# Seven-product expert steps: the third product is added on the sixth, the seventh and fourth go into the next step

## The chip, the cores and the metric

The kernel runs on one core of a Trainium2 chip. The metric is the time of one execution on the device in microseconds. The kernel before was run three times: 957.39, 956.89 and 956.15 us, median 956.89.

A core has several engines, each with its own in-order stream of instructions: TensorE (PE in the profile, its weight loads PEld), VectorE (DVE), ScalarE (ACT), GpSimd (POOL) and SyncE (SP, which issues DMAs). They meet at semaphores. TensorE writes its results to PSUM, which has eight banks; here they are called A, B, C, E and D0 to D3.

## The reference

One layer: cross-attention, then a feed-forward block with eight experts, each behind a layer norm and a residual.

```python
x = x + attention(layernorm(x), ctx)          # x: 16 x 112 x 256, ctx: 16 x 375 x 256
n = layernorm(x)                              # 1792 tokens of 256
g = einsum('bsh,ehf->ebsf', n, w_gate)        # 8 experts, 256 -> 1024
u = einsum('bsh,ehf->ebsf', n, w_up)
h = silu(g) * u
expert_out = einsum('ebsf,efh->ebsh', h, w_down)   # 1024 -> 256
cw = softmax(n @ w_router) * softmax((n @ w_gating) / 0.1)
cw = cw / (sum(cw) + 1e-9)
x = x + einsum('ebsh,bse->bsh', expert_out, cw)
```

All experts are computed for all tokens, in float32.

## The kernel before

The attention takes the first 110 us or so; a list scheduler written into the kernel (class `Line`) orders it, together with the very first expert step. Everything after that is emitted in the order of the code below, engine by engine.

**Steps.** The expert stage is cut into 128 steps (L303): eight experts, two halves of the tokens (896 each), four slices of 256 hidden features, and for each a gate step (even n, `m == 0`) and an up step (odd n, `up`). A step multiplies a 256 x 256 block of weights with 256 x 896 activations. It does so with seven products of 128 x 128 by 128 x 448 in place of eight, from sums of blocks made earlier (Winograd's form). Every product (`prod`, L444) is three float32r matmuls, high part by high, low by high and high by low, so a step has 21 matmuls of 448 columns. With Pi for product i, the four result blocks (token half T, feature half F) are

- (0,0) = P1 + P2
- W = P1 + P6, and (0,1) = W + P5 + P3
- U = W + P7, and (1,1) = U + P5
- (1,0) = U + P4

**Where the sums are made.** Matmuls add up in PSUM, but W is wanted in two sums and P5 in two. P1 goes to bank A; ACT copies it to B (L646), where P6 is added, which makes W. ACT copies W on to bank E (L656), where P7 and then P4 are added. VectorE copies W to SBUF as `w16` (L658). P5 goes to C; ACT copies it to SBUF as `p5` (L652), and P3 is added in C. VectorE then makes `c12 = w16 + C` (L671) and `c22 = p5 + E` (L676). TensorE's order in a step is P1, P5, P4 of the step before, P6, P2, P3, P7.

**What follows a step's results.** A gate step's blocks go through SiLU on ACT (`silu`, L463). An up step's blocks are multiplied into those on VectorE (`hide`, L522), cast to a high part on ACT (`hhi`) and the rest is formed on VectorE as a low part (`hlo`); `keep_hidden` (L480) casts at once and leaves the low part for later, `leave` (L515) leaves both. `carry` holds what is left for later under a name, and `finish` (L470) emits it at a chosen place of a later step.

**Down matmuls.** An up step queues 14 groups of three matmuls of 256 columns for the down projection (`queue_downs`, L715), and the next up step emits them, 4, 4 and 6 at a time, after its own products (`fill`, L454). They add up in D0 to D3 over the four slices, and `gather` (L431) takes a finished bank to the output with the routing weight. Groups 1 to 6 of an up step read token blocks T = 0 alone; the seventh is the first to read T = 1.

**Weights.** `begin` (L498) and `due` (L402) issue the weight loads (SP) and make their sums and low parts (POOL) some steps ahead; `hi` casts high parts on ACT in up steps.

Step 0 is in the attention's schedule, steps 1 to 5 follow hand-written scripts (`early_step`, L527), and `step` (L639) emits steps 6 to 127. What step 5 leaves over is put into `carry` by `left_over` (L608).

Of the kernel before, what the change touches and what calls it, by code (L numbers as in the profile page):

```python
# [143 lines left out]
def kernel(  # L144
# [17 lines left out]
    nc = tc.nc  # L162
# [3 lines left out]
    E, _, FF = w_gate.shape  # L166
# [10 lines left out]
    N = HT // 2  # L177
# [15 lines left out]
    def f(t):  # L193
        return t.bitcast(F32)

    def psum(tag, name):
        return pspool.tile([P, 512], F32, tag=tag, name=name)
# [14 lines left out]
    def buf(tag, shape, name, dtype=F32):  # L212
        if tag in AHEAD:
            fpool.tile([P, AHEAD.pop(tag)], F32, tag=f"ahead_{tag}", name=f"ahead_{tag}", bufs=1)
        return fpool.tile(shape, dtype, tag=tag, name=name, bufs=BUFS[tag])
# [87 lines left out]
    steps = [(e, h, j, m) for e in range(E) for h in range(NH) for j in range(NJ) for m in range(2)]  # L303
    PER = 2 * NJ
# [38 lines left out]
    def load_hi(k, part, copy=nc.scalar.copy):  # L343

        if k not in wts:
            t = buf("w", [P, 2, 7, P], f"w{k}", FR)
            wts[k] = (t[:, 0], t[:, 1])
        d, w = wparts(k)[part]
        copy(wts[k][0][:, d], w)  # L349
# [27 lines left out]
    for k in range(NW):  # L377
        e, i = divmod(k, PER)
        if e == 0:
            if i < EARLY:  # L380
                continue
            n = i - 2
            if i > EARLY:
                plan(n - 2, "raw", k)
        else:
            n = 2 * PER * (e - 1) + PER + (1, 3, 5, 5, 7, 9, 11, 13)[i]
# [3 lines left out]
        if k == EARLY:  # L390
            n = 1
        plan(n, "hi" if k != EARLY else "ghi", k)
        plan(n + 1, "lo", k)
    for q in range(E * NJ):
# [3 lines left out]
        n = (4, 6, 8)[j - 1] if e == 0 else 2 * PER * (e - 1) + PER + 2 * j + 9  # L398
# [3 lines left out]
    def due(n, what, *more):  # L402
        for k in todo.pop((n, what), ()):
            {"raw": load_raw, "rawd": load_rawd, "t": load_t, "lo": load_lo, "d": load_d,
             "hi": load_hi, "ghi": load_hi_slow}[what](k, *more)
# [5 lines left out]
    def down_group():  # L411

        n, h, q, fi, t, hs, first, last = downs.pop(0)
        e = q // NJ
        if (h, e) not in banks:
            banks[(h, e)] = {}
        bk_ = banks[(h, e)]
        opening = t // 2 not in bk_
        if opening:
            gather(t // 2)  # L420
            bk_[t // 2] = psum(f"D{t // 2}", f"pd{h}_{e}_{t // 2}")
        pd = bk_[t // 2][:, (t % 2) * D : (t % 2 + 1) * D]
        for s, (a, w) in enumerate(PASSES):
            nc.tensor.matmul(  # L424
                pd, hs[a][:, t * P : (t + 1) * P], wds[q][w][:, fi, :],
                start=(opening and s == 0), stop=(last and s == 2), skip_group_check=True,
            )
        if last:
            done.setdefault(t // 2, []).append((h, e, t, pd))

    def gather(bank, some=False):  # L431

        size = min(2, NTT - 2 * bank)
        if len(done.get(bank, ())) < (1 if some else size):
            return
        for h, e, t, pd in done.pop(bank):
            tt = h * NTT + t
            nc.vector.scalar_tensor_tensor(
                acc[tt], pd, cw[:, tt, e : e + 1], acc[tt], op0=ALU.mult, op1=ALU.add
            )  # L440
            if e == E - 1:
                (nc.scalar if h == NH - 1 and t == NTT - 1 else nc.sync).dma_start(out_f[tt * P : (tt + 1) * P, :], acc[tt])

    def prod(n, ps, i, start, stop):  # L444
        e, h, j, m = steps[n]
        w_ = wts[e * PER + 2 * j + m]
        xi, wi = PROD[i]
        for s, (w, a) in enumerate(PASSES):
            nc.tensor.matmul(  # L449
                ps, w_[w][:, wi, :], (xs_hi, xs_lo)[a][h][xi],  # L450
                start=(start and s == 0), stop=(stop and s == 2), skip_group_check=True,
            )

    def fill(k):  # L454
        for _ in range(min(k, len(downs))):
            down_group()
# [3 lines left out]
    def tmp(tag, n):  # L460
        return buf(tag, [P, N], f"{tag}_{n}")

    def silu(n, blk, src, own=True):  # L463
        s = src if own else tmp("s", f"{n}s{blk[0]}")
        nc.scalar.activation(s, src, AF.Silu)
        sg[blk] = s

    carry = {}

    def finish(*names):  # L470

        for name in names:
            if name in carry:
                carry.pop(name)()

    def parts(hid, blk):
        T, F = blk
        return [t[:, T * N : (T + 1) * N] for t in hid[F]]

    def keep_hidden(hid, blk):  # L480

        hi, lo = parts(hid, blk)
        s = sg[blk]
        nc.scalar.copy(hi, s)
        carry["hlo%d%d" % blk] = lambda: nc.vector.tensor_sub(lo, s, f(hi))
# [3 lines left out]
    def offer(n=1):  # L489

        while n and waiting:
            try:
                next(waiting[0])
                n -= 1
            except StopIteration:
                waiting.pop(0)

    def begin(n):  # L498

        for what in ("lo", "raw", "rawd", "t", "ghi"):  # L500
            due(n, what)
        hi_now = todo.pop((n, "hi"), ())

        def hi(part):
            for k in hi_now:
                load_hi(k, part)

        hid = None
        if n % 2:
            hid = [  # L510
                (buf("hhi", [P, HT], f"hhi{n}_{F}", FR), buf("hlo", [P, HT], f"hlo{n}_{F}", FR)) for F in range(2)
            ]
        return hi, hid

    def leave(hid, blk):  # L515

        hi, lo = parts(hid, blk)
        s = sg[blk]
        carry["hhi%d%d" % blk] = lambda: nc.scalar.copy(hi, s)
        carry["hlo%d%d" % blk] = lambda: nc.vector.tensor_sub(lo, s, f(hi))  # L520

    def hide(blk, src):  # L522
        nc.vector.tensor_mul(sg[blk], sg[blk], src)
# [115 lines left out]
    def step(n):  # L639
        e, h, j, m = steps[n]  # L640
        up = m == 1
        hi, hid = begin(n)

        pa, pb, pc = (psum(t, f"p{t}{n}")[:, :N] for t in "ABC")
        prod(n, pa, 1, True, False)
        nc.scalar.copy(pb, pa)  # L646
        if up:
            gather(2)
            gather(3)
        prod(n, pc, 5, True, False)  # L650
        p5 = tmp("v1", f"{n}p5")
        nc.scalar.copy(p5, pc)  # L652
        finish("fourth")
        prod(n, pb, 6, False, True)
        pe = psum("E", f"pE{n}")[:, :N]
        nc.scalar.copy(pe, pb)  # L656
        w16 = tmp("v1", f"{n}w")
        nc.vector.tensor_copy(w16, pb)  # L658
        finish("silu11")
        if up:  # L660
            due(n, "d")
        prod(n, pa, 2, False, True)
        if up:
            hide((0, 0), pa)
        else:
            silu(n, (0, 0), pa, False)
            finish("hhi01", "hhi11", "hhi10")
            due(n, "d")
        prod(n, pc, 3, False, True)
        c12 = tmp("s", f"{n}c12")  # L670
        nc.vector.tensor_add(c12, w16, pc)  # L671
        if not up:
            silu(n, (0, 1), c12)
        prod(n, pe, 7, False, False)
        c22 = tmp("s", f"{n}c22")
        nc.vector.tensor_add(c22, p5, pe)  # L676

        def fourth():
            prod(n, pe, 4, False, True)
            if up:  # L680
                hide((1, 0), pe)
                leave(hid, (1, 0))
            else:
                silu(n, (1, 0), pe, False)

        carry["fourth"] = fourth
        if up:
            keep_hidden(hid, (0, 0))
            hide((0, 1), c12)
            hide((1, 1), c22)  # L690
            fill(4)
            keep_hidden(hid, (0, 1))
            gather(0)
            finish("hlo00")
            hi(0)
            fill(4)
            if n == len(steps) - 1:
                finish("fourth")
            keep_hidden(hid, (1, 1))
            hi(1)  # L700
            gather(1)

            if n % PER != 1:
                finish("hlo01")
            offer(6)
            fill(6)
            queue_downs(n, hid)
        else:
            carry["silu11"] = lambda: silu(n, (1, 1), c22)
            finish("hlo00", "hlo01", "hlo11", "hlo10")  # L710
            hi(0)
            hi(1)
            offer(6)
# [618 lines left out]
    w16 = add("w", "v1", "B", "v1", ("first", "B"), waits=tail_s)  # L1332
# [5 lines left out]
    c22 = add("c22", "u", "C", u3, ("first", "C"))  # L1338
# [3 lines left out]
    c12 = add("c12", "w", "C", u3, c21, ("first", "C"), c22)  # L1342
# [40 lines left out]
    for n in range(1, len(steps)):  # L1383
# [7 lines left out]
            left_over(n, LEFT)  # L1391
        offer()
        assert not waiting
    finish("hlo01", "hlo11", "hhi10", "hlo10")
    while downs:
        down_group()
        for bank_ in range(4):
# [38 lines left out]
```

## Time and profile before

| | before |
|---|---|
| median of three runs | 956.89 us |
| the profiled execution | 957.04 us, span 955.3 us |
| TensorE busy | 948.3 us, 99% |
| VectorE busy | 655.5 us, 69% |
| ScalarE busy | 608.3 us, 64% |
| GpSimd busy | 377.4 us, 40% |
| copy of W to SBUF (L658) | 122 of 128 x 448, about 0.62 us each |
| copy of A to B (L646) | 122, 522 ns each |
| copy of B to E (L656) | 122, 517 ns each |

The span is the time from the first to the last instruction of the profiled execution; 1.7 us lie around it. A matmul of the expert stage starts 0.20 us after the one before it (448 columns) or 0.11 us (256 columns), while its own row is longer, since matmuls overlap. The trace's granted clock for TensorE is 0.999 of full speed. A row of the timeline gives start, duration, engine, line, operation and tiles; a bracket at its end says how long the engine had been idle and what ended that.

### The profile page before, as it was taken

To read this page: it belongs to the slowest core of one execution; us is meant where nothing else is said; L and a number is where in the kernel's file an instruction comes from. 1 tells how busy PE (TensorE), PEld (TensorE's weight loads), DVE (VectorE), ACT (ScalarE), POOL (GpSimd) and SP (SyncE) were. 2 spreads that over 40 slices of the span, in tenths; PEclk is the share of its full clock that TensorE was granted. 3 is DMA by queue.
4 is the path that set the end of the run, shared out by engine and by line. 5 is a ranking of instruction groups with operands and counts; after the bars stand their busy time and mean duration, and the time that the engine had idled before them with its cause. 6 is when DMAs were issued, how large, how long until landed. Compare 5 with 4: busy or idle time off the path is not lost.

```text
span 955.3 us, 16149 instructions
## 1 busy us (share of the span) xinstructions
PE 948.3 (99%) x6076; PEld 893.4 (94%) x6076; DVE 655.5 (69%) x1303; ACT 608.3 (64%) x1236; POOL 377.4 (40%) x481
## 2 busy tenths in 40 slices
PE   8999999999999999999999999999999999999998
PEld 5888999999999999999999999999999999999998
DVE  5878687777576666666575757667666767566675
ACT  5767776666666665666656666666666666666553
POOL 3437973344324433444244332543244431544000
PEclk9999999999999999999999999999999999999999
DMA  8621101011101110011101110111001110100001
GB/s 232 184 70 43 60 23 34 23 34 45 34 12 34 34 45 23 22 35 35 34 23 34 34 34 23 34 34 34 23 23 34 45 34 12 34 23 12 23 17 39
DMA packets 36577, 38.78 MB, mean 41 GB/s; under 512 B 3650, under 2 KB 34500, under 8 KB 36500
## 3 DMA queue, kind: packets, MB, share of 16 engines
q1 hardware_dynamic: 35808, 37.37, 13.3%
q8 instruction: 47, 0.77, 0.3%
q10 hardware_dynamic: 692, 0.40, 0.1%
q14 instruction: 30, 0.25, 0.1%
HBM read 34.08 MB, written 1.84 MB: 38 GB/s over the span
## 4 chain that ended last, share of the span: by engine, by line
PE 96%; DMA 1%; DVE 1%; ACT 1%; issue 0%; SPq 0%; ACTq 0%; DVEq 0%
PE pd L424 32%; PE pE L449 16%; PE pC L449 16%; PE pA L449 15%; PE pB L449 8%; PE ps_aa L1101 2%; PE ps_sc L1067 2%; PE ps_po L1116 1%; PE ps_cT L1055 1%; DMA wv<-in_L_xattn_Wv_dram 1%; PE ps_qk L1009 1%; PE ps_lg L1196 1%; PE ps_pp L1088 1%; DMA wn<-in_L_xattn_Wq_dram 0%; PE ps_xx L1163 0%
## 5 line engine op out<-in xcount | busy, mean ns | idle before, releaser
L424 PE MATMUL pd<-wd,hhi 128*128 128x256 f32 x1792 | 309.9, 277 | 0.0
L424 PEld LDWEIGHTS pd<-wd,hhi 128*128 128x128 f32 x1792 | 275.3, 188 | 2.0
L424 PE MATMUL pd<-wd,hlo 128*128 128x256 f32 x896 | 248.2, 277 | 0.4 <-DVE hlo L592 0.3
L449 PE MATMUL pC<-xs_hi,w 128*128 128x448 f32 x508 | 184.5, 363 | 0.0
L449 PE MATMUL pE<-xs_hi,w 128*128 128x448 f32 x508 | 184.1, 362 | 0.0
L359 POOL TENSOR_TENSOR w<-raw,w 128x384 fp32r<-128x384 f32 x64 | 78.3, 1223 | 265.3 <-ACT w L349 265.3
L449 PE MATMUL pA<-xs_hi,w 128*128 128x448 f32 x504 | 183.0, 363 | 0.0
L424 PEld LDWEIGHTS pd<-wd,hlo 128*128 128x128 f32 x896 | 168.3, 188 | 0.8 <-DVE hlo L592 0.8
L646 ACT COPY pB<-pA 128x448 f32<-128x448 f32 x122 | 63.6, 522 | 102.7 <-PE pA L449 102.7
L368 POOL TENSOR_TENSOR wd<-rawd,wd 128x512 fp32r<-128x512 f32 x32 | 41.8, 1306 | 182.0 <-ACT wd L366 182.0
L449 PEld LDWEIGHTS pC<-xs_hi,w 128*128 128x128 f32 x508 | 95.3, 188 | 10.4 <-DVE s_90c L671 0.4
L449 PEld LDWEIGHTS pE<-xs_hi,w 128*128 128x128 f32 x508 | 95.3, 188 | 6.3
L449 PEld LDWEIGHTS pA<-xs_hi,w 128*128 128x128 f32 x504 | 94.6, 188 | 5.5
L656 ACT COPY pE<-pB 128x448 f32<-128x448 f32 x122 | 63.1, 517 | 54.1 <-DVE s_4s L622 0.8
L449 PE MATMUL pC<-xs_lo,w 128*128 128x448 f32 x254 | 92.0, 362 | 0.0
L449 PE MATMUL pE<-xs_lo,w 128*128 128x448 f32 x254 | 91.8, 361 | 0.0
L449 PE MATMUL pB<-xs_hi,w 128*128 128x448 f32 x252 | 91.3, 362 | 0.0
L449 PE MATMUL pA<-xs_lo,w 128*128 128x448 f32 x252 | 90.9, 361 | 0.0
L359 POOL TENSOR_TENSOR w<-tt,w 128x512 fp32r<-128x512 f32 x64 | 88.5, 1382 | 0.0
L449 PEld LDWEIGHTS pE<-xs_lo,w 128*128 128x128 f32 x254 | 47.6, 187 | 3.3
L449 PEld LDWEIGHTS pB<-xs_hi,w 128*128 128x128 f32 x252 | 47.3, 188 | 3.1
L449 PEld LDWEIGHTS pC<-xs_lo,w 128*128 128x128 f32 x254 | 47.6, 187 | 2.5
(1456 smaller groups left out, 1779.0 us busy)
## 6 DMA issues: line engine op xcount, KB each, us to landing
raw<-in_L_ffn_w_gate_dram SPq DMA_DIRECT2D x32, 256.0 KB, 2.7
raw<-in_L_ffn_w_up_dram SPq DMA_DIRECT2D x32, 256.0 KB, 2.7
rawd<-in_L_ffn_w_down_dram SPq DMA_DIRECT2D x32, 256.0 KB, 2.7
ctx<-in_ctx_dram SPq DMA_DIRECT2D x13, 336.0 KB
out_dram<-acc SPq DMA_DIRECT2D x13, 128.0 KB, 1.7
wide<-in_ctx_dram SPq DMA_DIRECT2D x3, 336.0 KB, 7.5
wide<-in_x_dram SPq DMA_DIRECT2D x2, 448.0 KB
ctx<-in_ctx_dram SPq DMA_DIRECT2D x13, 39.0 KB
```

The lines of the kernel that those rows point to most:

```text
L359: nc.gpsimd.tensor_sub(wts[k][1][:, d], w, f(wts[k][0][:, d]))
L368: nc.gpsimd.tensor_sub(wds[q][1], rawds[q], f(wds[q][0]))
L424: nc.tensor.matmul(pd, hs[a][:, t * P : (t + 1) * P], wds[q][w][:, fi, :], start=(opening and s == 0), stop=(last and s == 2), skip_group_ ...
L449: nc.tensor.matmul(ps, w_[w][:, wi, :], (xs_hi, xs_lo)[a][h][xi], start=(start and s == 0), stop=(stop and s == 2), skip_group_check=True,)
L646: nc.scalar.copy(pb, pa)
L656: nc.scalar.copy(pe, pb)
L1009: nc.tensor.matmul(bank(("qk", g, m, 0), [P, GT]), m_b[k][a][:, m * P : (m + 1) * P], xnT_b[k][w], start=(k == 0 and s == 0), stop=(k == K ...
L1055: nc.tensor.transpose(bank(("cT", b, k), [P, TK])[:, c * KT : (c + 1) * KT], ct()[:, c, k * P : (k + 1) * P], ident[:KT, :KT],)
L1067: nc.tensor.matmul(bank(("sc", b), [TQ, TK]), own(qk_b[k], ("qk", g, k))[:, i * TQ : (i + 1) * TQ], ctT(k), start=(k == 0), stop=(k == KC ...
L1088: nc.tensor.transpose(bank(("pp", b), [KT, NK, TQ])[:, c, :], p()[:, c * KT : (c + 1) * KT], ident[:TQ, :TQ])
L1101: nc.tensor.matmul(bank(("aa", b), [P, KC, TQ])[:, k, :], ct()[:, c, k * P : (k + 1) * P], pT()[:, c, :], start=(c == 0), stop=(c == NK - 1),)
L1116: nc.tensor.matmul(bank(("po", b), [TQ, D]), aT()[:, a, k, :], (wv_hi, wv_lo)[w][:, k, :], start=(k == 0 and s == 0), stop=(k == KC - 1 an ...
```

## The change

P3 is added in bank B, on P1 + P6, instead of in C on P5. So `c12` becomes `p5 + B`, and the copy `w16` is gone. The bank that held P5 is then free: the copy of W goes there, and P7 and P4 are added there. This one bank, Z, is C in even steps and E in odd ones, so that P7 and P4 of a step can wait until the next: P7 is now emitted after the next step's P1 (with `c22` and what follows it), P4 before the next step's P3. TensorE's order is P1, P7 of the step before, P5, P6, P2, P4 of the step before, P3.

With them move the instructions that depend on them: the SiLU of (0,1) goes from the end of the gate step into the up step; the multiply and cast of (1,1) go from the up step into the next gate step; the casts and low parts of (1,0) and (1,1) go to the gate step after, or into the up step after that; gathers of D2 and D3 go from after P1 to after P6. The low part of (0,1) is always made in its own step. In the last step P7, P4 and what depends on them are emitted between the down groups.

```diff
@@ -639,75 +639,83 @@
     def step(n):
         e, h, j, m = steps[n]
         up = m == 1
+        end = n == len(steps) - 1
         hi, hid = begin(n)
 
-        pa, pb, pc = (psum(t, f"p{t}{n}")[:, :N] for t in "ABC")
+        pa, pb = (psum(t, f"p{t}{n}")[:, :N] for t in "AB")
         prod(n, pa, 1, True, False)
         nc.scalar.copy(pb, pa)
+        finish("silu01")
+        if up:
+            finish("hlo11")
+        finish("seven")
+        pz = psum("CE"[n % 2], f"pZ{n}")[:, :N]
+        prod(n, pz, 5, True, False)
+        p5 = tmp("v1", f"{n}p5")
+        nc.scalar.copy(p5, pz)
+        prod(n, pb, 6, False, True)
+        nc.scalar.copy(pz, pb)
+        finish("silu11")
         if up:
             gather(2)
             gather(3)
-        prod(n, pc, 5, True, False)
-        p5 = tmp("v1", f"{n}p5")
-        nc.scalar.copy(p5, pc)
-        finish("fourth")
-        prod(n, pb, 6, False, True)
-        pe = psum("E", f"pE{n}")[:, :N]
-        nc.scalar.copy(pe, pb)
-        w16 = tmp("v1", f"{n}w")
-        nc.vector.tensor_copy(w16, pb)
-        finish("silu11")
-        if up:
+            finish("hhi10")
             due(n, "d")
         prod(n, pa, 2, False, True)
         if up:
             hide((0, 0), pa)
+            finish("hlo10")
         else:
             silu(n, (0, 0), pa, False)
-            finish("hhi01", "hhi11", "hhi10")
+            finish("hhi11", "hlo00", "hlo01")
             due(n, "d")
-        prod(n, pc, 3, False, True)
+        finish("fourth")
+        prod(n, pb, 3, False, True)
         c12 = tmp("s", f"{n}c12")
-        nc.vector.tensor_add(c12, w16, pc)
-        if not up:
-            silu(n, (0, 1), c12)
-        prod(n, pe, 7, False, False)
-        c22 = tmp("s", f"{n}c22")
-        nc.vector.tensor_add(c22, p5, pe)
+        nc.vector.tensor_add(c12, p5, pb)
+
+        def seventh():
+            prod(n, pz, 7, False, False)
+            c22 = tmp("s", f"{n}c22")
+            nc.vector.tensor_add(c22, p5, pz)
+            if up:
+                hide((1, 1), c22)
+                leave(hid, (1, 1))
+            else:
+                carry["silu11"] = lambda: silu(n, (1, 1), c22)
 
         def fourth():
-            prod(n, pe, 4, False, True)
+            prod(n, pz, 4, False, True)
             if up:
-                hide((1, 0), pe)
+                hide((1, 0), pz)
                 leave(hid, (1, 0))
             else:
-                silu(n, (1, 0), pe, False)
-
-        carry["fourth"] = fourth
+                silu(n, (1, 0), pz, False)
+
+        carry.update(seven=seventh, fourth=fourth)
         if up:
             keep_hidden(hid, (0, 0))
             hide((0, 1), c12)
-            hide((1, 1), c22)
+            if end:
+                finish("seven", "hlo00")
             fill(4)
             keep_hidden(hid, (0, 1))
             gather(0)
             finish("hlo00")
             hi(0)
+            if end:
+                finish("hhi11", "fourth", "hlo01")
             fill(4)
-            if n == len(steps) - 1:
-                finish("fourth")
-            keep_hidden(hid, (1, 1))
             hi(1)
             gather(1)
-
-            if n % PER != 1:
-                finish("hlo01")
+            finish("hlo01")
+            if end:
+                finish("hhi10", "hlo11", "hlo10")
             offer(6)
             fill(6)
             queue_downs(n, hid)
         else:
-            carry["silu11"] = lambda: silu(n, (1, 1), c22)
-            finish("hlo00", "hlo01", "hlo11", "hlo10")
+            carry["silu01"] = lambda: silu(n, (0, 1), c12)
             hi(0)
             hi(1)
             offer(6)
@@ -1391,7 +1399,6 @@
             left_over(n, LEFT)
         offer()
         assert not waiting
-    finish("hlo01", "hlo11", "hhi10", "hlo10")
     while downs:
         down_group()
         for bank_ in range(4):
```

## The prediction

> **What bounds the kernel now.** I read the page's busy shares and its chain of waits first, to learn which engine sets the end.
>
> ```profile
> PE 948.3 (99%) x6076; PEld 893.4 (94%) x6076; DVE 655.5 (69%) x1303; ACT 608.3 (64%) x1236; POOL 377.4 (40%) x481
> ...
> PE 96%; DMA 1%; DVE 1%; ACT 1%; issue 0%; SPq 0%; ACTq 0%; DVEq 0%
> ```
>
> TensorE is busy throughout, and the chain that ends last is TensorE's own. A busy TensorE can still hide small gaps, so next comes the chain in order of time, in the middle of the expert stage.
>
> ```profile
> 479.04 4.78 PE pd L424 x42
> 483.82 0.60 PE pA L449 x3
> 484.42 0.60 PE pC L449 x3
> ...
> 488.02 0.61 PE pA L449 x3
> 488.63 0.60 PE pC L449 x3
> ...
> 491.63 0.61 PE pE L449 x3
> 492.24 4.79 PE pd L424 x42
> ```
>
> One pair of steps (gate and up) is 14 products of three matmuls and 42 down matmuls: 13.20 us from 479.04 to 492.24. Fourteen products at 0.60 and 4.78 for the downs give 13.18. So a pair holds about 0.02 us that is not matmul cadence. Over the whole stage the down groups start at 135.80 and, 60 pairs later, at 928.21: 13.207 each, so 0.027 x 60 = 1.6 us is all that better waiting could give back there. The changed function emits steps 6 to 127, 61 pairs. TensorE's list of waits confirms it; nothing in it belongs to these steps:
>
> ```profile
> PE ps_idle L815 <- DVE nhalf L223: 1.2, 1, 1.2
> PE ps_vb L923 <- ACT wide L1019: 1.0, 1, 1.0
> ...
> PE pd L424 <- DVE hlo L592: 0.3, 1, 0.3
> ```
>
> Last, the timeline from gate step 60 into up step 61, to see how late a result may come without delaying TensorE:
>
> ```profile
> 500.85 0.62 DVE L671 TENSOR_TENSOR s_60c<-v_60w,pC 128x448 f32<-128x448 f32 x1
> 501.07 0.36 PE L449 MATMUL pA<-xs_hi,w 128*128 128x448 f32 x1
> ...
> 501.46 0.37 PE L449 MATMUL pA<-xs_hi,w 128*128 128x448 f32 x1
> 501.51 0.58 ACT L465 ACTIVATE s_60c<-s_60c 128x448 f32<-128x448 f32 x1 [0.44 <-DVE s_60c L671]
> 501.67 0.37 PE L449 MATMUL pC<-xs_hi,w 128*128 128x448 f32 x1
> ...
> 501.99 0.53 ACT L646 COPY pB<-pA 128x448 f32<-128x448 f32 x1
> ...
> 502.88 0.36 PE L449 MATMUL pB<-xs_hi,w 128*128 128x448 f32 x1
> ```
>
> VectorE's sum over bank C ends at 501.47; the product that overwrites C starts at 501.67, 0.21 after the one before instead of 0.20. So **a result that ends 0.20 us ahead of its matmul is just in time**; this is the tightest edge of the old order. The copy into B ends at 502.52, 0.36 ahead of product 6, and costs nothing.
>
> **The change part by part.**
>
> *Removed:* the copy of B to SBUF (L658), 122 x 0.62 = 76 us of VectorE. It lies beside matmuls: 0 on the path. VectorE's cover falls from 69% to about 61%, so nothing is late next there.
>
> *TensorE's work:* the same 21 matmuls a step and 42 downs a pair, with the same weights: 0.
>
> *The new order, up step.* I lay it out from rows of before: product 0.60; a reader starts 0.40 after the start of a product's last matmul (501.46 would give 501.86; the first copy of a pair, matmul at 510.46 and copy at 510.86, shows it undisturbed); ACT 0.53, VectorE 0.62 with the next start 0.53 later; VectorE to ACT 0.04 to 0.09 (501.47 to 501.51; 512.68 to 512.77). Zero is the start of product 1; the order is 1, 7 of the gate step, 5, 6, 2, 4 of the gate step, 3.
> - Product 6 at 1.80 needs the copy A to B, and this now waits for the gate step's sum over B (product 3 has moved into B). Product 4's multiply on VectorE starts at -0.40 and lets go at 0.13; the sum runs 0.20 to 0.82, the copy 0.91 to 1.44. That is 0.36 ahead, 0.16 to spare, as before. Queued behind the copy on ACT are a SiLU and the copy of product 5, wanted only at 2.0.
> - Product 3 at 3.60 overwrites B, so it needs the copy B to bank Z: 2.60 to 3.13, 0.47 ahead.
> - Product 4 at 3.00 needs the sum after product 7 read: VectorE has the low-part subtraction first (0.73 to 1.35), then 1.40 to 2.02: 0.98 ahead. Even if that subtraction takes the 1.35 us that it takes in a few steps (481.87), the sum ends at 2.7, still 0.3 ahead.
> - The seventh down group, at 4.20 + 6 x 0.34 = 6.25, is the first to read the previous pair's low part of block (1,0), moved into this step behind its cast (3.6 to 4.15 on ACT): 4.20 to 4.82, over 1.4 ahead. A weight cast that shares this place (0.61 on ACT) comes after it in the queue.
> - The next gate step starts 4.8 us of downs later, with everything done. In it the SiLU on A (3.2 to 3.75) precedes the up step's product 1 at 4.20: 0.45 ahead, as now.
>
> So no edge is tighter than 0.36, and the edge at 0.20 (sum over C, then product 5) is gone, since C and E alternate. It costs 0.01 in each of 61 up steps, 0.6 us, and once more: from 699.46 to 700.18 two matmul starts are 0.41 and 0.31 apart instead of 0.20, 0.3 us, behind a late sum of step 90. **Gain 0.9 us**, bounds 0 and 1.6.
>
> *Step 6* is the first new step; it has no product 7 to issue, and its product 4 has moved back. So product 6 comes at 1.20, but the copy A to B runs 0.80 to 1.33 and wants 0.20 more: **0.33 us lost, once**.
>
> *The last step.* Product 7 ends at 4.80, four down groups follow, and product 4, moved ahead of the next four, would start at 6.17. VectorE must first do the low part (to 4.82), the sum over B (4.73 to 5.35), a multiply (5.26 to 5.87) and only then read Z, 5.79 to 6.41; plus 0.20, product 4 starts at 6.61: **0.44 us lost, once** (bounds 0 and 1.0, a further VectorE row or none in the queue). Ten down groups (3.4 us) then cover its multiply, cast and subtraction; the tail after them is as before.
>
> *Moved gathers, multiplies, SiLUs and casts:* each keeps its engine and its row, 0 on the path. In the 4.2 us of products ACT then has 5 instructions in a gate step and 7 in an up step, about 2.5 and 3.4 us, and VectorE 4 to 6, 2.1 to 3.2 us; the rest of an up step's work lies in 4.8 us of downs. Behind the low part at 4.20 VectorE's sum over B waits until 4.73, and behind that a multiply and a cast for the next pair. No DMA issue moves, and the SP and POOL queues keep their order.
>
> *A wait-only instruction on TensorE.* In the built program product 6 of each gate step from 8 on, 60 in all, is preceded by one, as it waits for VectorE and ACT. The expert stage of before has none, but the attention stage does:
>
> ```profile
> L1101 PEldq EVENT_SEMAPHORE  x1: 51/51/51, 31.5 to 31.5; - x1
> ```
> ```profile
> 31.44 1.49 PE L1101 MATMUL ps_aa<-s,ctx 125*128 125x112 f32 x12
> ```
>
> Upper bound 60 x 0.051 = 3.1 us. But these 12 matmuls, with the wait among them, start every (1.49 - 0.275) / 11 = 0.110 us, as the 24 at 25.56 do (2.67 us in all, 0.104 to 0.111 each). I take 0, by this nearest row; a product's matmul, at 0.20, leaves more room than one at 0.11. What the instruction waits for, VectorE's sum of the step before, ended more than 3 us earlier.
>
> [...]
>
> **The sum:** -0.9 + 0.33 + 0.44 = -0.13. The profiled execution took 957.04 us (span 955.3), 0.15 over the median of the three runs; so 956.9 against its own time and 956.8 as a median.
>
> **The rivals.** 0.2% (1.9 us) is about what a measurement of this kernel can tell from no change: below 955.0 or above 958.8.
> - *Product 6 of the up step comes late* (slower). Place: sum over B, copy A to B, product 6. It has 0.16 us to spare and decides from there: 0.20 beyond just-in-time (a sum that starts 0.36 late) gives 61 x 0.20 = 12 us, 969; a little over 0.03 is enough for 1.9 us. For it: two engines now follow each other between product 3 and product 6. Against it: both rows are fixed in length, 0.62 and 0.53, and the old order had the same 0.36.
> - *The 60 wait-only instructions are paid* (slower): 3.1 us, 959.8; from 0.03 each it counts. Against it: the row above.
> - *More is given back* (faster): all 1.6 us of the pairs and neither loss gives 955.3, still inside 0.2%. Beyond it the matmul cadence itself (0.200 and 0.113) would have to shrink. For it: 76 us less VectorE reading of PSUM beside the matmuls. Against it: product 1 takes 0.60 both at 483.82, where VectorE has nothing of its step to do yet, and at 488.02, amid its sums.
> - *76 us come off*, or a part of them, if VectorE were the bound: excluded by TensorE's 99%.
>
> **How the numbers follow.** No measurable change 0.70; late product 6 0.12 and paid waits 0.08, so slower 0.20; faster 0.10. Range: down to 955.0 (the 1.6 us and the noise: the three runs lie within 1.2 us); up to 960.2, past the paid waits. Left out are the late product 6 and most of the faster case, 2 in 10. Without rivals of either sign the forecast alone is 955.3 to 958.2: the bounds 0 and 1.6 on the gain, 0 and 1.3 on the two losses.
>
> **What would show it.** Right: pairs of 13.18 to 13.20 us between down groups; no L658 row; an idle gap before product 6 in step 6 and before product 4 in the last step, some 0.3 to 0.45 each; VectorE near 580 us busy. Wrong: pairs of 13.23 or more, and a gap before pB in up steps (late copy) or in gate steps (paid waits). What would make it wrong is a VectorE or ACT instruction that lasts longer in its new place than in its old one, ahead of the copy into B.

## The result: 0.1 to 0.3% slower, not the same

In the first comparison the changed kernel took 959.5 us (median of 8 executions, 958.19 to 961.46), the kernel before 956.39 (8 executions, 955.75 to 957.39): ratio 1.0027, 95% interval 1.0018 to 1.0037. The prediction said 956.8, range 955.0 to 960.2: the time lies in the range, but the likeliest case was no measurable change, and this is slower. A second comparison (below) gave 1.0015, 1.0002 to 1.0027. One remark is needed to read these: in some executions of every kernel that was run more than once the granted clock has a mean of 0.998 or 0.996, not 1.0, and they are 1.5 to 3 us longer; a single execution of the kernel before, 1754.59 us at a mean of 0.79, is left out everywhere.

The profiled execution of the changed kernel took 959.34 us, span 957.6 (before: 957.04 and 955.3). The page's busy shares and the shares of its chain of waits:

```profile
PE 950.8 (99%) x6076; PEld 898.4 (94%) x6076; DVE 619.3 (65%) x1181; ACT 598.1 (62%) x1236; POOL 378.4 (40%) x481
...
PE 96%; DMA 1%; DVE 1%; ACT 1%; issue 0%; SPq 0%; ACTq 0%; DVEq 0%
```

TensorE is the bound as before. Its own busy time is 2.5 us longer with the same 6076 matmuls, which is already a hint that it is not only waits that came. The chain in order of time, one pair of the changed kernel (start, length, what):

```profile
480.23 4.81 PE pd L424 x42
485.04 0.60 PE pA L449 x3
485.64 1.20 PE pZ L449 x6
486.84 0.60 PE pB L449 x3
...
492.84 0.60 PE pB L449 x3
493.44 4.81 PE pd L424 x42
```

The order is the new one (A, then 7 of the step before and 5 into Z, then B), and no product is longer than 0.60. But the 42 downs take 4.81 us where the rows of before have 4.78 and 4.79. A pair is 13.21 us. TensorE's list of waits has one new row:

```profile
PE ps_idle L823 <- DVE nhalf L223: 1.2, 1, 1.2
...
PE pd L424 <- DVE hlo L592: 0.3, 1, 0.3
PE pZ L449 <- DVE s_127c L680: 0.2, 1, 0.2
```

That is product 4 of the last step, as predicted. The other predicted loss, in step 6, is in the timeline (the bracket gives the idle time ahead and what ended it):

```profile
142.24 0.52 ACT L647 COPY pB<-pA 128x448 f32<-128x448 f32 x1 [0.19 <-PE pA L449]
...
142.44 0.37 PE L449 MATMUL pZ<-xs_hi,w 128*128 128x448 f32 x1
142.81 0.19 PEld L449 LDWEIGHTS pB<-xs_hi,w 128*128 128x128 f32 x1 [0.37 <-ACT pB L647]
142.81 0.47 PE L449 MATMUL pB<-xs_hi,w 128*128 128x448 f32 x1
```

Product 6 starts 0.37 after the matmul ahead of it in place of 0.20, and the next start is 0.11 late as well (0.31 in place of 0.20): 0.28 us. That is 0.05 behind the end of the copy (142.76) for the first start and 0.36 for the second.

**Where the 2.2 us between the two spans lie.** From the starts of the matmuls in both traces: the first product of the expert stage starts at 104.18 us, not 103.18, so 1.0 comes in the attention stage, which the change doesn't touch. From step 6 to the last matmul it is 812.87 us, not 811.56, so 1.31 comes in the steps that it does touch. The steps between and what follows the last matmul differ by less than 0.1. The 1.31 in parts, each a sum of distances between neighbouring starts (a gap is the lateness of a start that is over 0.03 us late):

| step 6 to the last matmul | before | after | difference |
|---|---|---|---|
| 2562 product matmuls, without gaps | 513.20 | 512.57 | -0.62 |
| 2520 down matmuls of the steps | 287.27 | 288.57 | +1.30 |
| gaps in products (before: at 699; after: 0.28 in step 6, 0.06 at 161, 0.21 at 305) | 0.32 | 0.55 | +0.23 |
| end: gaps | 0.34 | 0.80 | +0.46 |
| end: 87 matmuls | 10.44 | 10.38 | -0.05 |

(The rounded parts add up to 1.32.)

So two questions stood: is the 1.0 us in the attention stage the change's doing, and why do the same downs take 1.3 us longer?

### The profile page after: what moved, and what is told of

Its sections match the earlier page's. It is cut to its first block, busy times and chain, and to the rows that moved or that the text cites. A ratio compares the mean times of both kernels' runs of the same rounds, so it can differ in the third digit from the quotient of the medians.

```text
span 957.6 us, 16027 instructions
## 1 busy us (share of the span) xinstructions
PE 950.8 (99%) x6076; PEld 898.4 (94%) x6076; DVE 619.3 (65%) x1181; ACT 598.1 (62%) x1236; POOL 378.4 (40%) x481
## 4 chain that ended last, share of the span: by engine, by line
PE 96%; DMA 1%; DVE 1%; ACT 1%; issue 0%; SPq 0%; ACTq 0%; DVEq 0%
PE pd L424 32%; PE pZ L449 23%; PE pA L449 15%; PE pB L449 15%; PE ps_aa L1109 2%; PE ps_sc L1075 2%; PE ps_po L1124 1%; PE ps_cT L1063 1%; DMA wv<-in_L_xattn_Wv_dram 1%; PE ps_qk L1017 1%; PE ps_lg L1204 1%; PE ps_pp L1096 1%; DMA wn<-in_L_xattn_Wq_dram 0%; PE ps_xx L1171 0%; PE pE L449 0%
## 5 line engine op out<-in xcount | busy, mean ns | idle before, releaser
L449 PE MATMUL pZ<-xs_hi,w 128*128 128x448 f32 x732 | 246.2, 363 | 0.2 <-DVE s_127c L680 0.2
L449 PE MATMUL pB<-xs_hi,w 128*128 128x448 f32 x496 | 180.3, 363 | 0.0
L449 PEld LDWEIGHTS pZ<-xs_hi,w 128*128 128x128 f32 x732 | 137.4, 188 | 9.5 <-DVE s_127c L680 0.4
L449 PE MATMUL pZ<-xs_lo,w 128*128 128x448 f32 x366 | 131.8, 360 | 0.0
L449 PE MATMUL pB<-xs_lo,w 128*128 128x448 f32 x248 | 89.3, 360 | 0.0
L449 PEld LDWEIGHTS pZ<-xs_lo,w 128*128 128x128 f32 x366 | 68.4, 187 | 4.8
L657 ACT COPY pZ<-pB 128x448 f32<-128x448 f32 x122 | 63.1, 517 | 15.1 <-PE pB L449 0.4
L438 DVE SCALAR_TENSOR_TENSOR acc<-pd,cw,acc 128x256 f32<-128x256 f32 x112 | 48.3, 475 | 3.3 <-PE pd L424 3.3
L449 PEld LDWEIGHTS pA<-xs_lo,w 128*128 128x128 f32 x252 | 47.1, 187 | 2.5
L449 PEld LDWEIGHTS pB<-xs_lo,w 128*128 128x128 f32 x248 | 46.4, 187 | 3.2
```

The costliest lines, as they stand in the source:

```text
L438: nc.vector.scalar_tensor_tensor(acc[tt], pd, cw[:, tt, e : e + 1], acc[tt], op0=ALU.mult, op1=ALU.add)
L449: nc.tensor.matmul(ps, w_[w][:, wi, :], (xs_hi, xs_lo)[a][h][xi], start=(start and s == 0), stop=(stop and s == 2), skip_group_check=True,)
L657: nc.scalar.copy(pz, pb)
```

## The experiments

There are ten runs beside the first comparison: both kernels once more and eight variants, in three sessions, each on its own chip with its own executions of the kernel before.

### The attention stage: both kernels again

The trace of after has a stretch of half clock, 3.41 us long, in the attention stage (granted clock 0.50 between 65.9 and 69.1 us). The table by stretches of the changed kernel shows it in the column PEclk, 1.00 in the rows around it (length, then busy time of PE, PEld, DVE, ACT and POOL, the clock, DMA share, GB/s):

```profile
60.00:64.00 4.00, 4.00 (x39) 3.96 (x37) 3.66 (x15) 2.13 (x6) 1.10 (x2) 1.00 0.20 57
64.00:68.00 4.00, 4.00 (x31) 4.00 (x30) 2.94 (x12) 2.37 (x7) 2.34 (x3) 0.73 0.10 31
68.00:72.00 4.00, 4.00 (x18) 2.74 (x17) 2.57 (x7) 3.16 (x11) 1.42 (x3) 0.85 0.00 0
72.00:76.00 4.00, 4.00 (x39) 3.88 (x37) 3.96 (x13) 3.60 (x10) 2.29 (x3) 1.00 0.02 4
```

To tell whether it belongs to the change, the kernel before and the changed kernel were both run once more, unchanged.

> The kernel before, unchanged, to see how its attention stage and its granted clock vary from one execution to the next. Theory A (the attention stage varies by itself, and the changed kernel was unlucky there): times from 955.8 to 959 us, and in some executions a mean granted clock of 0.998 or 0.996, as in five of the eight of the changed kernel. Theory B (the change itself brings the half-clock stretch of the attention stage): no execution below 0.999, times 955.7 to 957.4, median 956.4. In both, a profile whose stage from step 6 to the last full set of downs lasts 787.6 us.

> The changed kernel, unchanged, beside the one before on the same chip. Theory A: ratio to the kernel before 1.0013, the 1.3 us that its expert stage took longer in the profile (0.3 in step 6, 0.5 in the last step, the rest in small pieces), with clocks spread as in the kernel before. Theory B: ratio 1.0025 to 1.0035 again, and a granted clock of 0.998 or less in half of the executions. In both, pairs of steps of 13.21 us.

Measured: before again 958.0 (12 executions, 956.19 to 960.12), ratio to its session's executions of before 1.001 (0.9999 to 1.0022); after again 958.14 (8, 957.38 to 960.48), ratio 1.0015 (1.0002 to 1.0027). Neither trace has half clock in the attention stage; the same stretch of after again:

```profile
64.00:68.00 4.00, 4.00 (x33) 3.52 (x32) 3.42 (x14) 3.21 (x9) 2.63 (x3) 1.00 0.10 31
68.00:72.00 4.00, 4.00 (x27) 3.03 (x26) 3.93 (x12) 3.81 (x11) 1.66 (x2) 1.00 0.01 4
```

The first expert product starts at 102.88 in before again and at 102.30 in after again. Over all twelve traces it starts at 104.18 to 105.93 in the four that have such a stretch (they are named at the end) and at 101.96 to 103.38 in the eight that have none. Put by the mean granted clock of each execution, over all sessions that list it:

| | clock 0.999 or 1.0 | 0.998 | 0.996 |
|---|---|---|---|
| before, 71 executions | 49, medians 956.6 to 957.0 | 14, 958.4 | 8, 959.8 |
| after, first comparison | 3, 958.3 | 3, 959.7 | 2, 961.1 |
| after again | 6, 957.7 | 2, 960.2 | 0 |
| three variants of it below, 35 | 30, medians 957.5 to 957.6 | 4, 959.0 to 959.9 | 1, 961.4 |

The kernel before has the low-clock executions too, 22 of 71, and the kernels with the new order not more often, 12 of 51. Theory A stands: of the first comparison's 3.1 us, 959.5 - 958.3 = 1.2 were the draw of the executions. Between executions of 0.999 and 1.0 in the second comparison, 957.73 is left against 956.66: **1.1 us, 0.11%**. In the first, where the clocks of before are not listed, it is 958.3 from three executions against 956.4; of these 1.9 us the 0.6 beyond the 1.31 of the steps stay unexplained. The stretch from step 6 to the last matmul repeats: 811.56 and 811.44 before, 812.87 and 812.94 after.

### Filling the two gaps

```diff
+        if n == max(SCRIPTS) + 1:
+            finish("fourth")
         prod(n, pb, 6, False, True)
...
             keep_hidden(hid, (0, 0))
+            if end:
+                finish("seven")
             hide((0, 1), c12)
             if end:
-                finish("seven", "hlo00")
+                finish("hlo00")
```

> The changed kernel with both one-time gaps closed: in step 6 the fourth product of step 5 goes ahead of the sixth as before, and in the last step VectorE's sum after product 7 goes ahead of the multiply of (0,1). Both theories: the gap of 0.27 us ahead of the sixth product of step 6 and the one of 0.46 us ahead of the fourth of the last step are gone from the profile, 0.73 us less in the expert stage. Theory A: ratio to the kernel before 1.0005. Theory B: 1.0018 to 1.0028, since the attention stage keeps its half-clock stretches.

Measured: 957.89 (11 executions), ratio 1.0015 (1.0006 to 1.0025); step 6 to the last matmul 812.61, so 0.26 less and not the 0.73 expected. The end's 0.46 is gone. Step 6's gap has only moved: product 3 now stands one product behind product 6 and waits for the copy of B to Z, as its chain in order of time shows (issue is time in which the engine waited for nothing that the profile shows, 0.04 us in the row below; ACTq, 0.02 us in a later chain, is ScalarE's sequencer):

```profile
141.68 0.61 PE pB L449 x3
...
142.38 0.53 ACT pZ L659
142.90 0.04 issue
142.95 0.88 PE pB L449 x3
```

So in the next version step 5's script leaves two groups of downs for that place:

```diff
-              ... downs:14 hhi:501 ...
+              ... downs:12 hhi:501 ...
...
+        if n == max(SCRIPTS) + 1:
+            fill(2)
         prod(n, pb, 6, False, True)
```

with the edit of the last step as above.

> The changed kernel with both of its gaps filled: two groups of downs that step 5 left out now stand ahead of step 6's product 6, and the last step takes product 7 ahead of the VectorE instruction that product 4 had to wait behind. Theory S (the 1.4 us that the expert stage lost are two parts, 0.27 + 0.46 = 0.73 us of gaps and a rest of some 0.7 us net that lies in the matmuls themselves: the first thirteen downs of a pair start over 1.611 us and not over 1.575): the gap ahead of step 6's product 6 falls from 0.27 us to under 0.05, the last step's 0.46 us goes, the stretch from step 6 to the last matmul falls from 812.9 us to 812.2, still 0.7 over the kernel before (811.5). Rival G (the gaps only cost what they are because something later waits in their place, and the rest is a set of small waits): closing them moves waits elsewhere, and the stretch stays above 812.6. The whole run: median 0.7 us under the changed kernel, so 957.4 to 957.7 where the kernel before has 956.9 to 957.

Measured: step 6 to the last matmul 812.86 with six downs in it that lay ahead of it before; without their 6 x 0.1133 it is 812.18. Median 957.6 (12 executions) against 956.92 on that chip, ratio 1.0004 (0.9994 to 1.0013). Both gaps are paid in full and both can be had back, 0.7 us. The other 0.6 us over before stay: they are in the matmuls.

### Why the same downs take longer

All 42 downs of a pair start 0.1133 us apart in the mean, except for the first thirteen behind the products. Counted from the start of the last product's matmul to the start of the thirteenth down, three values occur, 1.575, 1.595 and 1.611 us, and nothing between. They go with the starts that come before. Product matmuls start in a period of three (201, 198 and 202 ns, or a ns less); the value depends on where in that period the row ends (starts in ns; the bar is the first down):

```
1.575   201 198 201 | 201 117 118 117 116 114 113 113 113
1.595   197 202 201 | 203 116 116 119 118 118 122 116 114
1.611   202 201 197 | 204 117 118 114 117 120 120 118 118 122 116 114

pairs with      1.575   1.595   1.611
before             35      18       7
after               2       1      57
```

The mean over 60 pairs is 1.586 before and 1.609 after, 0.0238 x 60 = 1.4 us; that is the 1.3 of the table and 0.1 in the step from the last product to the first down, which the table counts with the products. In before, every one of the 60 pairs has one late product 5 in its up step (its first start 204 to 207 ns behind the last, 415 in the pair at 699), the just-in-time edge that the prediction wrote of; in the chain it is the product of 0.61:

```profile
448.43 0.60 PE pA L449 x3
449.03 0.61 PE pC L449 x3
449.64 0.60 PE pE L449 x3
...
452.64 4.78 PE pd L424 x42
```

In after no pair has it; three have a gap elsewhere (142, 161 and 305), and these three are the ones that don't read 1.611. So the theory: an undisturbed row of 42 ends in the slow place of the period, and a small wait in the row can put it elsewhere. It need not: 7 pairs of before read 1.611, and so do the three pairs with a gap in the kernel with the two finishes moved (the first under "Filling the two gaps"). That the place decides holds throughout: over all twelve traces, 720 pairs, the value is 1.611 where of the row's last three distances the short one (196 to 199 ns) is the last, 1.575 where it is the middle one and 1.595 where it is the first, with no exception. The first test put one or two matmuls of 64 columns ahead of product 1 of each up step (results overwritten by product 1); this is the kernel with one, the other has 2 for 1.

```diff
+        for _ in range(1 if up else 0):
+            nc.tensor.matmul(
+                pa[:, :64], wts[e * PER + 2 * j + m][0][:, W_B11, :], xs_hi[h][X_A11][:, :64],
+                start=True, stop=True, skip_group_check=True,
+            )
         prod(n, pa, 1, True, False)
```

> The changed kernel with one matmul of 64 columns more ahead of product 1 in every up step (its result is overwritten). Between them the 42 product matmuls of an up step repeat their starts with a period of three (0.201, 0.1975, 0.202 us). Theory S (how fast the first thirteen downs after the product run come depends on where in that period of three the run ends): one matmul more moves the period, so in most of the 60 pairs the thirteen downs take 1.575 or 1.595 us in place of 1.611. Rival (it depends on what ScalarE and VectorE do at that moment, or on the bank that the last product goes to): the sum stays at 1.611. The matmul itself costs between 0.03 us (a seventh of a product's matmul) and 0.13 us, 61 times, so 2 to 8 us on the run under either.

> The same with two matmuls of 64 columns more in every up step. Theory S: the period of three moves by another place, and the thirteen downs take another of the three sums (1.575, 1.595, 1.611) than with one matmul more. Rival: 1.611 as in the changed kernel. Cost of the two matmuls, 4 to 16 us under either.

Measured: 967.24 and 972.70 us (one execution each); 1.611 us in 58 and in 59 of 60 pairs. By the words of the expectation the theory fell. But the starts show that the test had not moved what it was to move: the row ends with 202, 201, 198 (or 197) and then 204 in both, as without them, since the period had begun anew behind the odd matmul and 21 is a multiple of three. What it showed is that in these two kernels the period counts from the last break. The second test therefore adds matmuls that are no break: full ones, 448 columns, one here and 2 in the other kernel.

```diff
+        for _ in range(1 if up else 0):
+            nc.tensor.matmul(
+                pa, wts[e * PER + 2 * j + m][0][:, W_B11, :], xs_hi[h][X_A11],
+                start=True, stop=True, skip_group_check=True,
+            )
```

> The changed kernel with one full matmul (448 columns) more ahead of product 1 in each up step; its result is overwritten. With a matmul of 64 columns there the period of three began anew behind it, so its place at the end of the run was the old one and nothing was told apart. Theory S2 (the period is counted from the last break in the row of 448-column matmuls, and how the thirteen downs come depends on how many such matmuls the row has, modulo three): 43 in a row leave 1, the last starts of the row read 201, 198, 202 ns, and the thirteen downs take 1.575 us (not 1.611) in most pairs. Rival (bank of the last product, or what ScalarE and VectorE do then): 1.611 as in the changed kernel. Cost 0.200 us x 61 = 12.2 us; under S2 12.2 - 60 x 0.036 = 10.0 us.

> The same with two full matmuls more. Theory S2: 44 in a row leave 2, the last starts read 198, 202, 201 ns, and the thirteen downs take 1.595 us. Rival: 1.611. Cost 0.400 x 61 = 24.4 us; under S2 24.4 - 60 x 0.016 = 23.4 us.

Measured: 971.29 and 983.78 us. With 43 in a row the thirteen downs take 1.575 us in 58 of 60 pairs, with 44 they take 1.595 in 59 of 60; step 6 to the last matmul grows by 10.07 and 23.39 us (expected 10.0 and 23.4). The rival falls: ScalarE, VectorE and the last product's bank are as in the changed kernel, and the value moves with the count alone. The chains in order of time, 43 first, 44 below:

```profile
459.54 4.78 PE pd L424 x42
472.92 4.78 PE pd L424 x42
```
```profile
463.83 4.79 PE pd L424 x42
477.43 4.79 PE pd L424 x42
```

A matmul more costs 0.20 to save 0.036, so the third test moves the row's end without one: the first two matmuls of each gate step's product 1 go ahead of the last group of downs, which leaves 40 in a row. It is built on the version with the gaps filled.

```diff
-    def prod(n, ps, i, start, stop):
+    def prod(n, ps, i, start, stop, split=False):
...
         for s, (w, a) in enumerate(PASSES):
+            if split and s == 2:
+                fill(1)
...
-        prod(n, pa, 1, True, False)
+        prod(n, pa, 1, True, False, not up and n > max(SCRIPTS) + 1)
...
-            fill(6)
+            fill(6 if end else 5)
```

> The kernel named closed (the changed one without its two gaps) in which the first two matmuls of product 1 of each gate step stand ahead of the last group of downs, so that 40 product matmuls (40 = 1 modulo 3) stand in a row ahead of the next downs. No matmul more. Theory S2: the thirteen downs take 1.575 in place of 1.611 us, 60 times, 2.2 us; the break that is added costs between nothing and what the break that is there costs (1.611 - 13 x 0.1135 = 0.135 us a pair, 8 us); the nearest row is three downs in it, which start 0.117, 0.118, 0.114 us behind each other in place of 0.1135, so 0.01 us a pair plus as much for the way back: 1 us. Forecast 1 us faster than closed: stretch of 811.2 us, about that of the kernel before. Rival: 1.611 stays, and the break costs on top, so slower than closed by 1 to 8 us.

Measured: 957.66 (12 executions), ratio 1.0004 (0.9994 to 1.0014); step 6 to the last matmul 812.93, beside 812.86 without the edit; the forecast was 811.2. The thirteen downs did go to 1.576 (59 of 60 pairs at 1.575), 0.033 a pair. The added break took the same back, as the timeline shows:

```profile
482.93 0.36 PE L451 MATMUL pA<-xs_hi,w 128*128 128x448 f32 x1
483.13 0.37 PE L451 MATMUL pA<-xs_lo,w 128*128 128x448 f32 x1
483.34 0.40 PE L424 MATMUL pd<-wd,hhi 128*128 128x256 f32 x2
483.57 0.29 PE L424 MATMUL pd<-wd,hlo 128*128 128x256 f32 x1
483.69 0.37 PE L451 MATMUL pA<-xs_hi,w 128*128 128x448 f32 x1
```

The three downs take 0.35 us (116, 116 and 123 ns a start) in place of 0.34, and the products behind them start 205, 203 and 206 ns apart: some 0.03 in all. The expectation had priced this break at 0.02. No version of the new order that was run beats the kernel before.

### One part alone: product 3 on B, in the old order

```diff
-        w16 = tmp("v1", f"{n}w")
-        nc.vector.tensor_copy(w16, pb)
...
-        prod(n, pc, 3, False, True)
+        prod(n, pb, 3, False, True)
         c12 = tmp("s", f"{n}c12")
-        nc.vector.tensor_add(c12, w16, pc)
+        nc.vector.tensor_add(c12, p5, pb)
```

> The kernel before with one part of the change alone: product 3 is added on B, behind product 6, its block is p5 + B, and the copy w16 is gone; order, banks C and E and the carried work as before. Product 3 then stands one product (1.2 us) behind product 6 and may write B only after ScalarE has copied B to E. Theory 1 (the steps had to be reordered because such a copy ends later than one product after its matmuls): a gap of about 0.33 us ahead of product 3 in each of some 121 steps, as in the one place of the kernel named ends where product 3 stands one product behind product 6 (0.22 + 0.11 us); 40 us, so 997 us. Theory 2 (the copy is just in time, and the reordering was for the balance of the engines): under 0.05 us a step, so under 963 us, and VectorE's share falls by the same as in the changed kernel, to some 65%.

Measured: 1000.76 us (one execution); step 6 to the last matmul 855.83, so 44.3 us more than before, 0.36 in each of 122 steps. VectorE falls to 592.1 us and it helps nothing. The chain in order of time goes through ScalarE in each step, at the copy of B that product 3 has to let pass. The lines below are an up step, 0.33 us late; in gate steps it is some 0.39, as there the copy also has to let VectorE's multiply of the block in E pass:

```profile
480.69 0.61 PE pB L449 x3
481.30 0.02 issue
481.32 0.02 ACTq L656
481.34 0.04 issue
481.38 0.53 ACT pE L656
481.90 0.04 issue
481.95 0.88 PE pB L449 x3
482.83 0.60 PE pE L449 x3
```

So the reordering is the price of dropping the copy to SBUF: with products 2 and 4 between 6 and 3 the same copy costs nothing, with product 2 alone it costs more than ten times all that the whole change lost.

## Why the prediction was wrong, by its own steps

- **The bound, the removed copy, "nothing is late next": right.** 36 us less of VectorE moved nothing. VectorE's own figure was wrong: 619.3 us, not near 580. The sum of its rows fell by 68 us from step 6 on, not 76: 35 of the 244 multiplies (L523) last over 0.9 us in their new place, where none did before, and 1 of the subtractions in place of 15. And neighbouring rows overlap on VectorE (0.62 long, 0.53 apart), so the union of them fell by 36 only. Third alone, without the new places, has 592.1.
- **The up step's timetable: right but for two steps.** One has a gap of 0.06 us, at 161. The timetable let VectorE's subtraction ahead of the sum after product 7 take up to 1.35 us and had that sum 0.3 ahead of product 4 even then. Here it takes 1.56 us, and the sum ends at 161.43, only 0.10 ahead:

```profile
159.34 1.56 DVE L520 TENSOR_TENSOR hlo<-s_6c,hhi 128x448 fp32r<-128x448 f32 x1
...
160.82 0.61 DVE L680 TENSOR_TENSOR s_8c<-v_8p,pZ 128x448 f32<-128x448 f32 x1
...
161.53 0.42 PE L449 MATMUL pZ<-xs_hi,w 128*128 128x448 f32 x1
...
161.80 0.36 PE L449 MATMUL pZ<-xs_lo,w 128*128 128x448 f32 x1
```

The other is the prediction's first rival, in one place. The sum over B starts 0.4 late there, the copy to B with it, and product 6 starts 0.10 late with 0.11 more behind it. Timeline of after:

```profile
304.53 0.62 DVE L675 TENSOR_TENSOR s_30c<-v_30p,pB 128x448 f32<-128x448 f32 x1 [0.40 <-PE pB L449]
...
305.24 0.52 ACT L647 COPY pB<-pA 128x448 f32<-128x448 f32 x1 [1.33 <-DVE s_30c L675]
...
305.51 0.37 PE L449 MATMUL pZ<-xs_hi,w 128*128 128x448 f32 x1
...
305.81 0.47 PE L449 MATMUL pB<-xs_hi,w 128*128 128x448 f32 x1
...
306.12 0.37 PE L449 MATMUL pB<-xs_lo,w 128*128 128x448 f32 x1
```

The late sum recurs, at the same place, in all nine traces of the new order; the late sum of step 90 in before, which the prediction counted as given back, is its like and is gone. So of "once more ... 0.3 us" 0.32 was won and 0.27 lost elsewhere (0.21 here, 0.06 at 161). Why one sum of 122 is late isn't settled. In the other up steps the copy into B ends 0.30 ahead of product 6, not 0.36, so 0.06 of the spare time was not there.
- **The just-in-time edge, 0.01 x 61 = 0.6: right, 0.62.**
- **Step 6, 0.33: 0.28. The last step, 0.44: 0.46.** Both right within 0.05; filling the gaps gave the 0.7 back. In the gaps shown the second matmul behind a late result starts 0.36 after its end (142.76 and 143.12, 305.76 and 306.12), so in these two a late result cost its lateness and 0.16; the prediction added 0.20.
- **The 60 wait-only instructions, 0: right.** Product 6 of a gate step starts 0.2017 us behind the matmul ahead of it, the mean of after, with such an instruction (60 rows of 51 ns in its trace), and 0.2016 in before, without one.
- **"TensorE's work: the same 21 matmuls a step and 42 downs a pair, with the same weights: 0": this is the step that failed.** It measured +1.30 us. The prediction took the matmul cadence as fixed (0.200 and 0.113) and called the 0.02 of a pair beyond it "all that better waiting could give back". But the downs of a pair are no fixed 4.78: they took 4.788 in the mean before and 4.810 after, since the first thirteen took 1.575, 1.595 or 1.611 us, according to how the row of products ended. By removing the small wait the change won 0.62 and lost twice that. The sum with the measured terms: -0.62 + 1.30 + 0.23 + 0.46 - 0.05 = 1.32; without the 1.30 it is 0.02, where the prediction had -0.13.
- **One reading was off.** Against the faster rival the prediction says that product 1 takes 0.60 at 483.82 and at 488.02. Its own line has 0.61 at 488.02: the late start of product 5.
- **The range** took the kernel's spread from three runs within 1.2 us. With the low-clock executions it is 955.7 to 960.7 for the kernel before alone, so single executions of 959.5 come without the change; but no session's median of before is above 958.0.

The pairs, 13.21, fell between the two signs that the prediction had set (13.18 to 13.20 right, 13.23 wrong). An effect of 1.3 us is 0.02 a pair, so the second sign was set too far off to show it.

What stays open: which place a given wait leads to is known in part. Counting the matmuls behind the row's last late start (204 ns or more), modulo three, gives the value as with 42, 43 and 44 in all 60 pairs of the kernel with product 3 alone moved, and in 42 of the 60 of before; the other 18, with one late start of 206 or 207 ns, read 1.595. Putting before's just-in-time wait back into the new order was not tried. What makes the half clock come is open as well.

## What to carry to other kernels

When TensorE is 99% busy, a change of order has to be counted in the starts of single matmuls, not in waits: the pace behind a switch of shapes is a term of its own (here 1.575 to 1.611 us for the first thirteen matmuls of 256 columns behind those of 448), and a tiny wait may pay for itself there, as the one of before seems to have done (0.01 us in each up step, beside 0.0238 a pair in those thirteen). Before a difference of a few tenths of a per cent is explained, compare the same stage in two executions of each kernel and sort the executions by their granted clock; here more than a third of the first difference had nothing to do with the change. And an accumulation that is moved onto a bank which another engine still copies needed its distance in products here: one product between them was 0.33 us short in up steps and 0.39 in gate steps, two were enough (in after, for one, a copy of B ends at 488.05 and product 3 starts at 488.48).

## What the runs showed of the hardware

- The expert stage's matmuls of 448 columns in a row started in a period of three, 201, 198 and 202 ns or a ns less. With the place in it where the row ended went, in all 720 pairs of the twelve traces, whether the next thirteen matmuls of 256 columns took 1.575, 1.595 or 1.611 us (13 x 0.1133 = 1.473 is their own pace). So the switch cost 0.10 to 0.14 us.
- A matmul of 64 columns in a row of 448-column ones cost 0.11 to 0.12 us (6.8 us for 61 of them, 14.1 for two each), about as much as one of 256 columns (0.1133).
- A stretch of half clock of 3.41 us came in the first 70 us of four of the twelve traced executions: at 65.8 in after and near 18 in the kernels with one odd matmul, with 43 and with 44 in a row, and in none of the other eight traces. The four executions have a mean clock of 0.998, which is what one such stretch makes of it: 3.41 x 0.5 us in 957 is 0.0018. All four are of the new order (nine traces; three are of the old), but the stage is untouched and the kernel before has such mean clocks as often. Between 17 and 23 us of the kernel with 43 in a row:

```profile
17.00:20.00 3.00, 2.65 (x11) 1.91 (x12) 0.72 (x3) 1.30 (x3) 3.00 (x5) 0.76 0.75 201
20.00:23.00 3.00, 3.00 (x8) 1.58 (x7) 1.33 (x6) 0.00 (x0) 1.45 (x2) 0.67 1.04 277
```
